# A fused attention and causal-convolution kernel: where the sums of weights and of outputs stand among a softmax's steps, and where its reciprocal and division stand

## The chip, the cores and the metric

The kernel runs on one core of a Trainium2 chip. A core has a matrix engine (TensorE, PE in the profile; PEld is its weight load), a vector engine (VectorE, DVE), a scalar engine (ScalarE, ACT), a general engine (GpSimd, POOL) and a queue engine that issues DMAs (SyncE, SP). Each runs its own instructions in order and waits for the others by semaphores. The metric is device time in microseconds, the median of several runs. Everything is float32.

## The reference

For four sequences (b) of 1024 tokens with 1024 channels and 16 heads of 64:

```python
scale, shift = split(cond @ W_emb + b_emb)             # one row a sequence
xn  = rms_norm(x, g_norm) * (1 + scale) + shift
q, k, v = heads(xn @ W_qkv)                            # (b, 16, 1024, 64)
q, k = rms_norm(q, g_q), rms_norm(k, g_k)
o   = softmax(q @ k.T / 8) @ v                         # heads joined again
x   = x + (o + o @ W_out)
x   = x + causal_conv(x, taps=cond, bias=b)            # depthwise, 4 taps
```

The last layer takes the four rows of cond as the taps of a depthwise convolution over tokens.

## The kernel before

**Products.** Both large products (with W_qkv and with W_out) are done as two-by-two blocks in seven multiplications instead of eight, which needs sums and differences of blocks. Those of x go to DRAM as scrA (L326), those of W_qkv as scrB (class Weights, combine, L565, four subtractions of 128x384 for each of four row blocks of a double), those of W_out as scrW (class OutWeights: diagonals L908, two of 128x128, and combine L916, four of 128x512), those of o as scrS (class OutSums, combine, L942, four of 128x512). In this document "a lot" is one such group of two or four instructions on DVE. A later load (w_P, wq_P, o_P) brings the results back.

**Stages.** A "double" is two pairs of heads: 28 pieces of four matmuls (L648), each into a PSUM tile of the pool ps_m, which has three buffers in turn. DVE and ACT empty such tiles (L658 to L669); qk is scaled on DVE (L498) and transposed on PE (L506). The same three buffers serve qkt, the transposes of x (xtp), the output product's po and pe (L1046, emptied for example by L1058, L1077 and L1080), and the sums' tot (L767).

**Units.** A unit is one pair of heads and one half of the queries; there are 64, 16 a sequence. Its steps: eight score tiles on PE (L689), copied by ACT to sp (L697); eight maxima, of which seven instructions on DVE (L706); the maximum over partitions on POOL (L711); its copy to PSUM by ACT (mbp, L720); eight shifts on DVE (L725); eight exponentials on ACT (L729); seven additions of the exponentials on POOL (L731); and in the next unit's time the product with v (pav, L752, a PSUM tile with one buffer), the total over partitions (tot, L767), then the reciprocal and the division. The reciprocal's way: ACT copies tot to tots (L785), a DMA spreads it over 128 partitions as few (L787), DVE takes the reciprocal of 128x8 (L790), a DMA writes it to DRAM (scrR, L792), and two DMAs read it back as rec (L795), each row of it on 64 partitions. The division oT = pav * rec follows on DVE (L804) and a DMA stores it (L811).

**Order.** For PE, DVE, ACT and POOL, the order of instructions on an engine is the order in which the Python code issues them. A model clock orders it: `tick(us)` advances it by the time of PE's work, `defer(delay, key, step)` runs a step once the clock has passed, and `need(key)` runs at once whatever still waits under a key. The `softmax` method (L733) of a unit sets, counted from its call: the maximum over partitions at 2.6 (TO_MAX), the copy at 6.5 (TO_SPREAD), shift kt at 7.6 + kt times 1.8 (TO_SHIFT, STEP; 1.6 in the first sequence), the exponential 1.3 behind it. `finish` (L763) defers the copy of tots by 0.2 and `invert` (the reciprocal and its two DMA steps) by 6.0; this is called one pair of score tiles before `softmax`. `divide` is deferred by DIVIDE = 15.0 from `softmax`.

Work without a due time of its own, the lots (but for the first few) and most scalings of qk, is handed in with `defer_gap`. `fill_gap(GAP)` takes what is ripe, scalings of qk first, up to 6.5 us by estimate, and is called at TO_MAX + 0.1, while POOL takes the maximum.

SP issues all DMAs, in an order of its own; a DMA at the head of its queue that waits holds back the ones behind it.

Of the kernel before, what the change touches and what calls it, by code (L numbers as in the profile page):

```python
# [21 lines left out]
def kernel(  # L22
# [69 lines left out]
    clock = [0.0]  # L92
# [3 lines left out]
    def defer(delay, key, step):  # L96
        pending.append((clock[0] + delay, next(serial), key, step))

    def flush(due):
        while True:  # L100
            ready = [e for e in pending if due(e)]
            if not ready:
                return
            entry = min(ready, key=lambda e: e[:2])
            pending.remove(entry)
            entry[3]()

    def tick(us):

        clock[0] += us  # L110
        flush(lambda e: e[0] <= clock[0])
# [4 lines left out]
    idle, loud = [], [0.0, 0.0]  # L116
# [3 lines left out]
        pending.append(entry)  # L120
        idle.append((clock[0] + delay, us, entry))

    def fill_gap(us):
        for e in sorted(idle, key=lambda e: e[2][2][0] != "qk"):
            if e[2] not in pending:
                idle.remove(e)
            elif e[0] <= clock[0] and e[1] <= us:
                us -= e[1]
                idle.remove(e)
                pending.remove(e[2])  # L130
                e[2][3]()
# [8 lines left out]
    def need(*key):  # L140
        flush(lambda e: e[2] == key)
# [535 lines left out]
    class Unit:  # L677
# [55 lines left out]
        def softmax(self):  # L733

            key = ("exp", self.name)
            loud[0] = clock[0] + TO_SHIFT + TO_EXP
            step = STEP if self.pr.b else STEP_FIRST
            loud[1] = loud[0] + NT * step + LOUD
            defer(TO_MAX, key, self.maximum)
            defer(TO_MAX + 0.1, key, lambda: fill_gap(GAP))  # L740
            defer(TO_SPREAD, key, self.broadcast)
            for kt in range(NT):
                at = TO_SHIFT + kt * step
                defer(at, key, lambda kt=kt: self.shift(kt))
                defer(at + TO_EXP, key, lambda kt=kt: self.weigh(kt))
# [15 lines left out]
        def finish(self):  # L761
            b, c = self.pr.b, self.pr.c
            tot = ps_m.tile([P, HN], F32, tag="m", name=f"tot_{self.name}")  # L763
            for g in range(4):
                h, i = divmod(g, 2)
                some = slice(0, HN) if self.final else slice(i * QN, (i + 1) * QN)
                nc.tensor.matmul(  # L767
                    tot[32 * g : 32 * (g + 1), : some.stop - some.start],
                    ones,
                    self.sum[:, h, some],  # L770
                    start=True,
                    stop=True,
                )
            tick(2 * PAIR)
            self.tot = tot
            if self.final:
                return
            key = ("tot", self.name)
            defer(0.2, key, lambda: self.spread(tot))
            defer(6.0, key, self.invert)  # L780

        def spread(self, tot):

# [417 lines left out]
    TO_MAX, TO_SPREAD, TO_SHIFT, TO_EXP, STEP = 2.6, 6.5, 7.6, 1.3, 1.8  # L1201
# [1 line left out]
    SHARES = (0.25, 0.5, 0.25)  # L1203
    LEADS = ((11, 7), (10, 9))
    LEADS_LAST = ((11, 7), (10, 12))
    DIVIDE = 15.0
    STEP_FIRST = 1.6
    BEHIND_FIRST = 22.0
    LATER = ((0, 0), (4, 0))
    GAP = 6.5  # L1210
    AGE = 30.0
    LOUD = 5.0
    PB = NJ // 2
# [182 lines left out]
    def between(p):  # L1396

        b, i = divmod(p, NB)
        slots = [[] for _ in range(7)]
        for j in range(7):  # L1400
            T = 7 * (p + 4) + j
            slots[j] = piece(T) if T < ND * NPR + 16 else []
        slots[0].append((0.0, lambda: store(AGE)))
        d, k = divmod(p - 11, NB)
        if 0 <= d < B - 1 and k % 2 == 0 and k < NJ:
            slots[0].append((0.0, lambda: OutSums(d, k // 2).load()))
        if p < NB + 1:
            for i in PLAN.get(p, ()):
                slots[0] += [(0.0, lambda: load_step(i)), (0.0, lambda: load_o(i))]
        if p == NB + 1:  # L1410
            for load in (lambda: load_step(KH), lambda: load_o(KH), lambda: load_step(KH + 1)):
                slots[0].append((0.0, load))
        for a, pieces in enumerate(out_steps(p)):
            slots[(2, 5)[a] if NB < p < B * NB - 4 else 6] += pieces
        if p == B * NB - 4:
            slots[0].append((0.0, lambda: held.load(0, 0)))
            slots[0].append((0.0, lambda: held.load(1, 0)))
            slots[6].append((0.0, lambda: defer(1.0, ("S3",), held.differences)))
        if p == B * NB - 2:
            slots[6].append((0.0, lambda: defer(5.0, ("o2",), lambda: held.load(0, 1))))  # L1420
            slots[6].append((0.0, lambda: defer(5.0, ("o2",), lambda: held.load(1, 1))))
            slots[6].append((0.0, lambda: defer(11.0, ("S1",), lambda: held.sums((0, 1), range(KH - 1)))))
        if p == B * NB - 1:
            slots[6].append((0.0, lambda: defer(1.0, ("S4",), lambda: held.sums((2,), range(KH - 1)))))
        return [piece for slot in slots for piece in slot]
# [19 lines left out]
    def split(pieces, behind):  # L1445

        left, n = behind, len(pieces)
        while n and left > 0:
            n -= 1
            left -= pieces[n][0]  # L1450
        return cut(pieces[:n], SHARES) + [pieces[n:]]
# [38 lines left out]
    last = None  # L1490
    for p in range(B * NB):
        unit = Unit(doubles[p // 4].pairs[p // 2 % 2], p % 2)
        stretches = split(between(p), BEHIND if p else BEHIND_FIRST)
        stretches = iter(stretches)

        def fill():
            run(next(stretches))

        if last is not None:
            need("exp", last.name)  # L1500
            last.values(range(0, HT))
        unit.scores((0, 1))
        fill()
        if last is not None:
            last.values((4, 5))
        unit.scores((2, 3))
        fill()
        if last is not None:
            last.values((6, 7))
        unit.scores((4, 5))  # L1510
        fill()
        if last is not None:
            last.finish()
        unit.scores((6, 7))
        need("mx", unit.name)
        unit.softmax()
        if last is not None:
            defer(DIVIDE, ("oT", last.pr.b, last.pr.c, last.half), last.divide)
        fill()
        last = unit  # L1520
# [45 lines left out]
```

## Time and profile before

| what | value |
|---|---|
| median of 3 runs | 2849.01 us (2847.79 to 2849.99) |
| the profiled execution | 2850.03 us, span 2848.2 us |
| PE busy | 2744.6 us, 96% of the span |
| DVE busy | 2217.1 us, 78% |
| ACT, POOL busy | 1539.2 us, 1325.5 us |
| chain that ended last | PE 72%, DVE 14%, DMA 7% |
| mean TensorE clock granted | 0.993 |
| POOL's additions, L731 | 384 of 2.44 us, 64 of 2.37 us in the mean |
| shifts, L725 | 512 of 1.21 us |
| division, L804 | 64, median 0.683 us |

How to read it: busy time counts an engine's instructions that run, not those that wait, issue DMAs or handle semaphores. In a timeline, a row has the start, the length, the engine, the line, what is written and read, the shape and the number of instructions merged in it; in brackets stands the engine's idle time before the row and what ended it. A group of a tile's view has the least, the median and the greatest length of one instruction in ns. In a table of windows, the columns are the busy time of each engine with the number of its instructions, then the granted share of TensorE's clock, the DMA engines' busy share and GB/s.

### The profile page before, as it was taken

To read this page: it belongs to the slowest core of one execution; us is meant where nothing else is said; L and a number is where in the kernel's file an instruction comes from. 1 tells how busy PE (TensorE), PEld (TensorE's weight loads), DVE (VectorE), ACT (ScalarE), POOL (GpSimd) and SP (SyncE) were. 2 spreads that over 40 slices of the span, in tenths; PEclk is the share of its full clock that TensorE was granted. 3 is DMA by queue.
4 is the path that set the end of the run, shared out by engine and by line. 5 is a ranking of instruction groups with operands and counts; after the bars stand their busy time and mean duration, and the time that the engine had idled before them with its cause. 6 is when DMAs were issued, how large, how long until landed. Compare 5 with 4: busy or idle time off the path is not lost.

```text
span 2848.2 us, 31740 instructions
## 1 busy us (share of the span) xinstructions
PE 2744.6 (96%) x10533; PEld 1304.7 (46%) x10533; DVE 2217.1 (78%) x2623; ACT 1539.2 (54%) x2208; POOL 1325.5 (47%) x534
## 2 busy tenths in 40 slices
PE   6999999999999999999999999999999999999978
PEld 3544444444444444444444445444444444443334
DVE  4587787877887887878788778777887887788786
ACT  4255656655555656655555556665454545555532
POOL 2055544554455544544554555354455445544520
PEclk9999999999999999999999999999999999999999
DMA  9854556655545655754554556565456444534554
GB/s 322 272 167 144 192 165 206 215 180 173 172 164 173 207 188 186 243 171 165 188 196 158 172 196 194 189 210 194 152 176 218 140 146 163 170 126 137 174 155 122
DMA packets 420503, 518.31 MB, mean 182 GB/s; under 512 B 40884, under 2 KB 323572, under 8 KB 410996
## 3 DMA queue, kind: packets, MB, share of 16 engines
q1 hardware_dynamic: 420340, 516.29, 55.5%
q8 instruction: 84, 1.38, 0.2%
q14 instruction: 79, 0.65, 0.1%
HBM read 417.63 MB, written 98.30 MB: 181 GB/s over the span
## 4 chain that ended last, share of the span: by engine, by line
PE 72%; DVE 14%; DMA 7%; ACT 3%; issue 2%; SPq 1%; POOL 0%; DVEq 0%; ACTq 0%; POOLq 0%
PE pqkv_P L648 28%; PE pav L752 15%; PE s L689 14%; DVE mx L706 5%; PE po_P L1046 5%; PE po L1046 4%; DVE sp L725 2%; DVE qk L498 2%; DMA rec<-scrR 2%; PE pe_P L1046 1%; DMA scrR<-few 1%; PE qkt L506 1%; ACT sp L697 1%; DVE S L942 1%; DMA we<-in_L_cond_W_emb_dram 1%
## 5 line engine op out<-in xcount | busy, mean ns | idle before, releaser
L648 PE MATMUL pqkv_P<-w_P,a 128*128 128x384 f32 x3456 | 1178.0, 491 | 29.2 <-issue 6.6
L731 POOL TENSOR_TENSOR sum<-sum,sp 128x1024 f32<-128x1024 f32 x384 | 936.8, 2440 | 42.5 <-ACT sp L729 13.3
L648 PEld LDWEIGHTS pqkv_P<-w_P,a 128*128 128x128 f32 x3456 | 641.2, 191 | 494.3 <-issue 80.6
L697 ACT COPY sp<-s 128x1024 f32<-128x1024 f32 x512 | 501.4, 1016 | 495.3 <-PE s L689 494.9
L729 ACT ACTIVATE sp<-sp 128x1024 f32<-128x1024 f32 x512 | 533.3, 1055 | 229.1 <-DVE sp L725 224.3
L725 DVE TENSOR_TENSOR sp<-sp,mbp 128x1024 f32<-128x1024 f32 x512 | 607.2, 1211 | 27.2 <-ACT mbp L720 27.2
L711 POOL PARTITION_ALL_REDUCE mb<-mx x64 | 219.7, 3433 | 852.5 <-DVE mx L706 454.0
L706 DVE TENSOR_TENSOR mx<-mx,sp 128x1024 f32<-128x1024 f32 x384 | 484.8, 1262 | 126.6 <-ACT sp L697 96.3
L689 PE MATMUL s<-qT,kT 64*128 64x512 f32 x2048 | 510.6, 617 | 3.1 <-ACT sp L697 3.1
L752 PE MATMUL pav<-sp,v 128*64 128x512 f32 x2048 | 482.0, 602 | 4.3 <-DVE oT L804 4.3
L731 POOL TENSOR_TENSOR sum<-sp,sp 128x1024 f32<-128x1024 f32 x64 | 151.4, 2366 | 483.7 <-ACT sp L729 223.7
L689 PEld LDWEIGHTS s<-qT,kT 64*128 64x128 f32 x2048 | 175.8, 186 | 307.6 <-ACT sp L697 143.2
L1169 DVE SCALAR_TENSOR_TENSOR y<-x,cols,y 128x512 f32<-128x512 f32 x192 | 276.6, 1444 | 16.1 <-ACT y L1157 11.5
L752 PEld LDWEIGHTS pav<-sp,v 128*64 128x64 f32 x2048 | 130.4, 136 | 322.6 <-issue 292.9
L706 DVE TENSOR_TENSOR mx<-sp,sp 128x1024 f32<-128x1024 f32 x64 | 109.7, 1714 | 161.2 <-ACT sp L697 161.1
L1046 PE MATMUL po_P<-o_P,wq_P 128*128 128x512 f32 x352 | 158.3, 594 | 6.7 <-DMA o_P<-scrS 2.6
L667 DVE TENSOR_TENSOR qk<-u,pqkv_P 128x256 f32<-128x256 f32 x256 | 105.4, 412 | 76.0 <-PE pqkv_P L648 76.0
L498 DVE TENSOR_TENSOR qk<-qk,ms 128x1024 f32<-128x1024 f32 x64 | 136.0, 2145 | 0.0
L1046 PE MATMUL po<-o_P,wq_P 128*128 128x512 f32 x288 | 129.8, 593 | 2.8 <-DMA o_P<-scrO 1.8
L720 ACT COPY mbp<-mb 128x1024 f32<-128x1024 f32 x64 | 65.1, 1017 | 117.8 <-POOL mb L711 117.8
L1157 ACT ACTIVATE y<-x,cols,tap_self 128x512 f32<-128x512 f32 x64 | 52.1, 813 | 119.4 <-DVE x L1080 117.5
L1046 PEld LDWEIGHTS po_P<-o_P,wq_P 128*128 128x128 f32 x352 | 65.6, 190 | 81.2 <-issue 66.3
(118 smaller groups left out, 1810.4 us busy)
## 6 DMA issues: line engine op xcount, KB each, us to landing
a<-scrA SPq DMA_DIRECT2D x212, 512.0 KB
w_P<-scrB SPq DMA_DIRECT2D x64, 768.0 KB
o_P<-scrS SPq DMA_DIRECT2D x44, 1024.0 KB
w_P<-in_L_cond_W_qkv_dram SPq DMA_DIRECT2D x192, 192.0 KB
o_P<-scrO SPq DMA_DIRECT2D x29, 1024.0 KB
wq_P<-scrW SPq DMA_DIRECT2D x108, 256.0 KB
scrA<-r SPq DMA_DIRECT2D x28, 896.0 KB
xc<-in_x_dram SPq DMA_DIRECT2D x64, 256.0 KB
```

The costliest lines, as they stand in the source:

```text
L498: nc.vector.tensor_mul(qk, qk, self.ms[g].unsqueeze(2).to_broadcast([P, 4 * HT, D]))
L648: nc.tensor.matmul(pm, (chunk.r(place) if a is None else a[:, k, :])[:, t % 2 * P : (t % 2 + 1) * P], w[:, k, :], start=(k == 0), stop=(k ...
L689: nc.tensor.matmul(ps[:, h, :], pr.kT[kt // HT][h * D : (h + 1) * D, kt % HT * P : (kt % HT + 1) * P], pr.qT[self.half][h * D : (h + 1) * ...
L697: nc.scalar.copy(sp, ps)
L706: nc.vector.tensor_max(self.mx, self.mx if kt > 1 else self.sp[0], self.sp[kt])
L711: nc.gpsimd.partition_all_reduce(self.mb.rearrange("p h q -> p (h q)"), self.mx.rearrange("p h q -> p (h q)"), P, bass_isa.ReduceOp.max,)
L725: nc.vector.tensor_sub(self.sp[kt], self.sp[kt], self.mb)
L729: nc.scalar.activation(sp, sp, AF.Exp)
L731: nc.gpsimd.tensor_tensor(self.sum, self.sum if kt > 1 else self.sp[0], sp, ALU.add)
L752: nc.tensor.matmul(self.pav[h * D : (h + 1) * D, :], self.pr.v[kt // HT][:, kt % HT, h * D : (h + 1) * D], self.sp[kt][:, h, :], start=(kt ...
L1046: nc.tensor.matmul(pm, self.w[name][:, k, :], self.operand(name, k), start=start and k == 0, stop=k == KH - 1)
L1169: nc.vector.scalar_tensor_tensor(self.y, self.x1[:, k : k + HN], cols[:, r : r + 1], self.y, ALU.mult, ALU.add)
```

## The change

```diff
-    def fill_gap(us):
-        for e in sorted(idle, key=lambda e: e[2][2][0] != "qk"):
+    def fill_gap(us, scales):
+        for e in list(idle):
             if e[2] not in pending:
                 idle.remove(e)
-            elif e[0] <= clock[0] and e[1] <= us:
+            elif e[0] <= clock[0] and e[1] <= us and (e[2][2][0] == "qk") == scales:
...
-            defer(TO_MAX + 0.1, key, lambda: fill_gap(GAP))
+            defer(TO_MAX + 0.1, key, lambda: fill_gap(GAP, True))
+            defer(TO_SHIFT + 2.0 * STEP + 0.1, key, lambda: fill_gap(GAP, False))
...
-            defer(6.0, key, self.invert)
+            defer(9.0, key, self.invert)
...
-    DIVIDE = 15.0
+    DIVIDE = 12.0
...
-    GAP = 6.5
+    GAP = 5.0
...
         need("mx", unit.name)
+        if last is not None:
+            need("tot", last.name)
         unit.softmax()
```

`fill_gap` is now called twice in a unit: at the old place for scalings of qk alone, and 0.1 behind the due time of the third shift for everything else, with 5.0 us by estimate each. The `need("tot")` ahead of `softmax` issues the reciprocal and its DMA steps directly behind the eighth maximum of the next unit, before anything that `softmax` defers; the 9.0 of `finish` is thus never reached there. The division comes due at 12.0 instead of 15.0 behind `softmax`, which is behind the third shift instead of the fifth, and behind the lots where there are any.

The order of instructions, compared engine by engine, is the same on PE, ACT and POOL; it differs on DVE and SP. In the first sequence and a little beyond, each of the first 19 units held one or two lots ahead of its first shift; after the change 16 of the first 18 hold one or two, behind the third shift (the first unit's behind the first). In the second and third sequence, four lots of o each stood in every second unit (eighth maximum at 1260.9, 1343.2 and so on) and now stand one unit earlier (1221.0, 1304.2 and so on), behind the third shift.

## The prediction

> **What bounds the kernel now.** I read the page first, then the waits of TensorE and of VectorE, then the timelines of single units. The page says that TensorE is busy nearly all the span:
>
> ```profile
> PE 2744.6 (96%) x10533; PEld 1304.7 (46%) x10533; DVE 2217.1 (78%) x2623; ACT 1539.2 (54%) x2208; POOL 1325.5 (47%) x534
> ```
>
> So 2848.2 - 2744.6 = 104 us are idle on PE, and a change that adds no PE work can win part of that at most. In the windows of 100 us, PE is busy 92.7 to 97% between 100 and 900 us, and 96.5 to 100% from 900 to 2700. Other engines matter only where they make PE wait, and VectorE (DVE) is the one that does, because it empties PE's PSUM tiles. Among DVE's own waits this one belongs to the change:
>
> ```profile
> DVE oT L804 <- DMA rec<-scrR: 52.4, 20, 5.0
> ```
>
> The division waits 20 times for the reciprocals' way through DRAM. The timeline of DVE shows how in a unit that holds sums (I name a unit by the end of its eighth maximum; here 1260.9):
>
> ```profile
> 1260.82 4.05 DVE L498 TENSOR_TENSOR qk<-qk,ms 128x1024 f32<-128x1024 f32 x2
> 1264.80 2.86 DVE L942 TENSOR_TENSOR S<-S 128x512 f32<-128x512 f32 x4
> 1267.57 0.20 DVE L790 RECIPROCAL few<-few 128x8 f32<-128x8 f32 x1
> 1267.68 1.17 DVE L725 TENSOR_TENSOR sp<-sp,mbp 128x1024 f32<-128x1024 f32 x1
> ...
> 1273.82 1.21 DVE L725 TENSOR_TENSOR sp<-sp,mbp 128x1024 f32<-128x1024 f32 x1
> 1278.32 0.69 DVE L804 TENSOR_TENSOR oT<-pav,rec 128x512 f32<-128x512 f32 x1 [3.29 <-DMA rec<-scrR]
> ```
>
> The reciprocal stands behind the sums, 6.7 us after the maximum; the issues of scrR and rec follow at 1268.36 and 1272.79, between loads, and DVE idles 3.29 us with three shifts queued behind the division. The change takes this stall away.
>
> **What goes.** "tots" is copied and "few" issued 2.5 us ahead of the eighth maximum's end (1258.44 here), and where the reciprocal stood first after it, at +0.4 us, it didn't wait. So moved forward it costs its 0.19 us and no wait. Of SP's queue: scrR (0.4 us) and the two rec issues (0.6 each) move up some 3 to 6 us past one or two loads of w_P and a, which PE releases anyway; where nothing lay between, SP went from scrR to rec in 1.4 us (scrR's landing); rec landed 5.5 us after its first issue here, so at some +7.5 us, and the division comes at +9 or later. I take the 52.4 us of DVE's wait as gone (both ends: all of it, or half if the queue is full). What that is worth on PE: in eleven units the trace has a PE gap at +17 to +22 us (starts of matmuls against their usual spacing), behind the late division or the shifts that it held up (1.43, 1.25, 0.74, 1.49, 0.87, 0.61, 1.59, 0.43, 1.96, 1.91, 1.21), 13.5 us in all. In the first batch, sums ahead of the first shift also hold up DVE's emptying of PSUM: at 656.95 PE waited 1.69 us for u of L660, which stood behind 4.9 us of W sums. Gaps of this kind there are about 14 us; I take 8. **Gain 21.5 us** (bounds 13 and 27).
>
> **What comes.** PE's, ACT's and POOL's orders stay as they are; DVE's and SP's change. Sums stood ahead of shift 0, while POOL ran its all-reduce (3.25 us), and there one of them took 0.69 us. Now they stand behind shift 2. The nearest rows for what they meet there are these two groups of the same shape, both with two SBUF inputs:
>
> ```profile
> L942 DVE TENSOR_TENSOR S<-S x48: 677/692/2385, 616.4 to 2180.2; 128x512 f32<-128x512 f32 x48
> L853 DVE TENSOR_TENSOR S<-o,o x4: 776/2840/2853, 2601.3 to 2607.5; 128x512 f32<-128x512 f32 x4
> ```
>
> The four of L853 are the only ones that ran beside POOL's additions (L731, 2.37 us each): three took 2.84 us, waiting out one addition apiece. The shifts (an input in PSUM) take 1.21 us beside POOL and without. When do the additions start? In every unit at +10.4 to +12.8 us. Behind the third shift of a unit that is the moment the sums arrive. But POOL has only two additions to do until shift 3 is through, as the third needs its exponential. So a lot of four costs 4 x 0.69 = 2.8 us of work plus up to two waits of 2.1, **7 us**.
>
> Worked out for the unit at 1221.0, which now holds the S lot that the unit at 1260.9 held:
>
> ```profile
> 1231.20 1.21 DVE L725 TENSOR_TENSOR sp<-sp,mbp 128x1024 f32<-128x1024 f32 x1
> 1232.33 0.68 DVE L1077 TENSOR_TENSOR ou<-ou_P,po_P 128x512 f32<-128x512 f32 x1
> 1232.92 2.34 DVE L725 TENSOR_TENSOR sp<-sp,mbp 128x1024 f32<-128x1024 f32 x2
> 1235.19 0.68 DVE L804 TENSOR_TENSOR oT<-pav,rec 128x512 f32<-128x512 f32 x1
> 1235.79 0.41 DVE L667 TENSOR_TENSOR qk<-u,pqkv_P 128x256 f32<-128x256 f32 x1
> ```
> ```profile
> 1231.33 2.37 POOL L731 TENSOR_TENSOR sum<-sp,sp 128x1024 f32<-128x1024 f32 x1 [6.88 <-ACT sp L729]
> ```
> ```profile
> 1230.93 5.32 PE L648 MATMUL pqkv_P<-w_P,a 128*128 128x384 f32 x16
> 1236.09 0.60 PE L506 MATMUL qkt<-ident,qk 128*128 128x128 f32 x4
> 1236.53 2.78 PE L648 MATMUL pqkv_P<-w_P,a 128*128 128x384 f32 x8
> ```
>
> POOL has begun at 1231.33, before shift 2 ends at 1232.4. The lot ends near 1238.7, then oT 0.6, then L1077 until 1239.9 instead of 1233.0. It empties the PSUM tile whose buffer (three of ps_m, in turn) the transposes at 1236.09 take: PE waits 3.7 us. Then two shifts, and L667 ends at 1242.5 (before 1236.3) for the product at 1236.53: 2 us more. Together 6.
>
> A unit where shift 2 ends before POOL starts is better off: at 1304.2 shift 2 ends at +8.8 and POOL starts at +10.6, so three sums are free and one waits: x of L1080 is 3.7 us late, with 2.1 to spare, PE waits 1.7. Done so for each unit that now holds sums, shift 0 moved up to the end of the broadcast copy where sums had held it: 1.0, 3.4, 5.1, 3.5, 5.1, 1.0, 4.8, 7.4, 5.8, 4.4 in the first batch (units at 140, 213, 254, 367, 408, 487, 531, 572, 690, 727; the other first-batch lots stay within their cover) and 6.4, 1.7, 5.8, 1.7, 5.8, 2.1, 5.4, 2.5 in the later two (every second unit from 1221 to 1508.6 and 1889.6 to 2174.9; a few steps of 0.2 included). That is **73 us**. If each lot met one addition only, ten of these would be 2 to 3 us smaller: 43. I take the middle, **58**, as both the start of POOL and who gets in first at the meeting are uncertain by about one sum.
>
> A long PE gap costs more. At 230.03 PE had idled 3.07 us, and the next eight matmuls took 5.46 us instead of the 2.75 of other rows of eight:
>
> ```profile
> 230.03 5.46 PE L648 MATMUL pqkv_P<-w_P,a 128*128 128x384 f32 x8 [3.07 <-DVE sp L725]
> ...
> 229.00:236.00 7.00, 5.97 (x10) 2.82 (x12) 3.79 (x6) 3.87 (x7) 6.76 (x4) 0.52 1.03 318
> ```
>
> The granted clock is 0.52 in that stretch and 0.66 at 317 to 322, after a gap of 2.47 us; after 1.69 us (656.95) it stays 1.00. Of the gaps above, twelve exceed 2.5 us, and two of these units pay already: 10 x 2.6 = 26 us at most; for the middle case I count six, **16 us** (8 at the low end). The Trainium skill ("TensorE: Matmul & The Clock Gate", part 1) halves the clock after an idle window of about 3.4 us that runs free of the work; by it, an estimate, gaps of 2.5 us would mostly go free and this term would be about half. The row at 317 speaks against that.
>
> **Sum**: 58 + 16 - 21.5 = +52 us on the profiled execution's 2850.0 (span 2848.2), 2902; the runs' median is 1 us lower: **2901 us**. Bounds: 73 + 26 - 13 = +86 and 43 + 8 - 27 = +24, so 2935 and 2873.
>
> **The rivals.** (1) *The sums go through together*: they stand 0.03 us apart, and if DVE runs a lot without a break and POOL waits instead, a lot costs 2.8 us less the 0.7 of the division that leaves its old place. The slacks of PSUM tiles in these stretches are 0.1 to 4.6 us, so PE loses perhaps 0.5 us in each of the 24 units that hold sums, 12 us, against 21.5 gained: 2850.0 - 9.5 is 2840. It decides from a PE loss below 0.9 us a unit. For it: the 0.03 us gaps. Against: L853, whose sums stand as close, and the taps of L1169, which take 2.7 us beside POOL and 0.75 alone. Chance 0.13. (2) *The cover is better than I read it*: DVE idles between the shifts and the next scores (1.52 us at 1242.37), few gaps reach 2.5 us, the gains are whole: +0 to +22, about 2862. Chance 0.15, of which 0.07 lies within 0.2%. (3) *The reciprocal waits for few*: behind it stand qk scaling and PSUM's emptying. Landing 1 us after the maximum would cost up to 0.5 us of PE in 63 units, +30 on top: about 2930. Against it: no wait in the trace at +0.4. Chance 0.05. My forecast has 0.67.
>
> Slower by over 0.2% (about what a measurement of this kernel can tell from no change): 0.67 + 0.05 + 0.08 = 0.80; within: 0.07; faster: 0.13. The range, 2858 to 2935, leaves out rival 1 and the smallest losses.
>
> **What would show it.** Right: sums of L565, L916 and L942 near 2.5 us in mean where two meet POOL, the wait of oT for rec nearly gone, PE gaps of 2 to 6 us at +12 to +18 in the units named, and stretches with a clock of about 0.5 behind them. Wrong: sums at 0.69 us, or an unchanged PE beside late DVE work, or a wait of the reciprocal for its DMA.

## The result, and the profile after

The changed kernel takes **2929.2 us** in the median of 4 runs (2924.4 to 2932.7), the kernel before, run beside it, 2849.5 (2847.8 to 2850.6): a ratio of 1.0279, 95% interval 1.0261 to 1.0297. The forecast was 2901 with a range of 2858 to 2935. The time came out slower, as forecast, and inside the range, but +80 us where the sum gave +52. One run of the kernel before, in the last set of runs, took 3589 us at a mean clock of 0.782; it is left out of all comparisons here.

The profiled execution took 2929.29 us, its span is 2927.5. The page's line of busy times:

```profile
PE 2772.1 (95%) x10533; PEld 1317.2 (45%) x10533; DVE 2283.5 (78%) x2623; ACT 1544.0 (53%) x2208; POOL 1346.2 (46%) x534
```

Against before, PE is busy 27.5 us more with the same 10533 matmuls (a lower clock: mean 0.98 against 0.993), and idle 155.4 us instead of 103.6. So of the span's +79.3, 51.8 are new idle time and 27.5 slower matmuls. DVE is busy 66 us more with the same 2623 instructions: the sums have become longer by 33.7 us in all, the maxima (L706), which have two SBUF inputs as well, by 26.3. The groups of the same shape as before's L942 and L916 (one line lower now; least, median, greatest in ns):

```profile
L943 DVE TENSOR_TENSOR S<-S x48: 684/692/2821, 611.1 to 2220.6; 128x512 f32<-128x512 f32 x48
L917 DVE TENSOR_TENSOR W<-W x16: 685/692/2828, 563.0 to 782.1; 128x512 f32<-128x512 f32 x16
```

Most are still 0.69 us. The long ones are few, and come at most twice in a lot. The unit that stood at 1221.0 has its eighth maximum at 1269.0 now. Its DVE, POOL and PE timelines:

```profile
1268.90 0.20 DVE L791 RECIPROCAL few<-few 128x8 f32<-128x8 f32 x1
...
1279.14 1.22 DVE L725 TENSOR_TENSOR sp<-sp,mbp 128x1024 f32<-128x1024 f32 x1
1280.27 6.49 DVE L943 TENSOR_TENSOR S<-S 128x512 f32<-128x512 f32 x4
1286.67 0.68 DVE L805 TENSOR_TENSOR oT<-pav,rec 128x512 f32<-128x512 f32 x1
1287.27 0.68 DVE L1078 TENSOR_TENSOR ou<-ou_P,po_P 128x512 f32<-128x512 f32 x1
1287.87 2.35 DVE L725 TENSOR_TENSOR sp<-sp,mbp 128x1024 f32<-128x1024 f32 x2
1290.13 0.42 DVE L667 TENSOR_TENSOR qk<-u,pqkv_P 128x256 f32<-128x256 f32 x1
1290.46 0.28 DVE L667 TENSOR_TENSOR v<-u,pqkv_P 128x128 f32<-128x128 f32 x1
```
```profile
1279.64 2.35 POOL L731 TENSOR_TENSOR sum<-sp,sp 128x1024 f32<-128x1024 f32 x1 [7.17 <-ACT sp L729]
1282.08 2.68 POOL L731 TENSOR_TENSOR sum<-sum,sp 128x1024 f32<-128x1024 f32 x1
1290.32 4.81 POOL L731 TENSOR_TENSOR sum<-sum,sp 128x1024 f32<-128x1024 f32 x2 [5.57 <-ACT sp L729]
```
```profile
1278.95 5.32 PE L648 MATMUL pqkv_P<-w_P,a 128*128 128x384 f32 x16
1288.01 0.66 PE L506 MATMUL qkt<-ident,qk 128*128 128x128 f32 x4 [3.73 <-DVE ou L1078]
1290.84 5.25 PE L648 MATMUL pqkv_P<-w_P,a 128*128 128x384 f32 x8 [2.18 <-issue]
```

The lot of four takes 6.49 us: 2.28, 2.72, 0.69 and 0.69. It waits out what is left of POOL's first addition and then the second, which in turn runs 0.33 us late (2.68 against 2.35); the third addition can't come, because shift 3 stands behind the lot. PE waits 3.73 us for the tile that L1078 empties, and 2.18 us more until just behind the end of L667 at 1290.74 (the profile names no releaser there), where the prediction had 3.7 and 2. The next eight products take 5.25 us instead of 2.75. This unit is 8.8 us longer.

What the change was to take away is gone: the division's wait for rec (52.4 us, 20 times) is in no row of DVE's waits, and the reciprocal never waited (L791, mean 196 ns). In DVE's list another wait has grown; columns are total, times and longest, here of the kernel after:

```profile
DVE mx L706 <- ACT sp L697: 255.3, 123, 11.7
DVE qk L667 <- PE pqkv_P L648: 87.8, 60, 7.0
DVE sp L725 <- ACT mbp L720: 61.7, 51, 4.2
```

The first shift waits 61.7 us for the broadcast maximum, where it was 27.2 us, 28 times, before. That is the cover under which the lots used to run, now left empty.

The lengths of the units (end of one eighth maximum to the next) add up as follows, in us against before's trace. "Eight lots" are the units at 1221, 1304, 1388, 1470, 1890, 1972, 2055 and 2137, which hold a lot in the changed kernel; "eight freed" are the ones that follow them, which held it before. "Last three units" are those at 2582, 2626 and 2668. Stretches that change little are left out, so a row's parts need not reach its span. The rows below the first belong to the experiments. A row is one execution: those of "after, additions short", "lots back, reciprocal early" and "lots back, division late" are the fastest of their runs, 3, 7 and 7 us below the medians given further on.

| kernel (profiled execution) | first 18 units | eight lots | eight freed | last three units | behind the last maximum | span |
|---|---|---|---|---|---|---|
| after | +46.2 | +31.6 | -9.0 | +10.2 | -3.3 | +79.3 |
| before, additions short | -12.4 | -0.4 | +2.4 | -3.2 | -10.9 | -20.5 |
| after, additions short | -22.0 | +9.3 | -7.7 | +3.2 | -8.3 | -24.4 |
| lots back, reciprocal early | -4.2 | +0.7 | -8.0 | +10.8 | -3.1 | -0.6 |
| lots back, reciprocal early, division late | -5.8 | +1.2 | -8.2 | +8.6 | -4.5 | -5.6 |
| lots back, reciprocal early but for the last four units | -2.1 | 0.0 | -6.7 | +4.6 | -2.8 | -5.5 |
| lots alone | +34.0 | +33.6 | -9.2 | +3.1 | -1.9 | +60.1 |
| the change but for the last four units | +49.9 | +30.4 | -9.0 | -0.3 | 0.0 | +74.3 |
| lots behind the eighth shift | +14.0 | +12.5 | -10.0 | +12.2 | -2.7 | +31.7 |
| lots behind the second shift | +16.1 | +19.9 | -10.1 | +9.7 | -1.3 | +40.6 |
| early reciprocal in eight units | -9.8 | +0.2 | -7.3 | +2.5 | +0.9 | -11.2 |

The eight lots differ, and their units with them. Four lots (units at 1221, 1388, 1890, 2055) met additions: they took 4.94 to 6.92 us, and their units became 5.8 to 8.8 us longer, 29.5 in all. The other four (1304, 1470, 1972, 2137) stood behind the same shift but ended before POOL began: they took 2.87 us, and their units became 0.3 to 1.1 us longer, 2.1 in all.

### The profile page after: what moved, and what is told of

Same layout as the page of the kernel before. It is cut to its first block, busy times and chain, and to the rows that moved or that the text cites. A ratio compares the mean times of both kernels' runs of the same rounds, so it can differ in the third digit from the quotient of the medians.

```text
span 2927.5 us, 31695 instructions
## 1 busy us (share of the span) xinstructions
PE 2772.1 (95%) x10533; PEld 1317.2 (45%) x10533; DVE 2283.5 (78%) x2623; ACT 1544.0 (53%) x2208; POOL 1346.2 (46%) x534
## 4 chain that ended last, share of the span: by engine, by line
PE 70%; DVE 17%; POOL 3%; issue 3%; DMA 3%; ACT 3%; SPq 1%; DVEq 0%; POOLq 0%; ACTq 0%
PE pqkv_P L648 31%; PE s L689 12%; PE pav L753 12%; DVE mx L706 5%; PE po_P L1047 5%; PE po L1047 4%; DVE sp L725 3%; DVE y L1170 2%; POOL sum L731 2%; PE qkt L506 1%; PE pe_P L1047 1%; DVE r L326 1%; POOL mb L711 1%; PE tot L768 1%; DMA we<-in_L_cond_W_emb_dram 1%
## 5 line engine op out<-in xcount | busy, mean ns | idle before, releaser
L648 PE MATMUL pqkv_P<-w_P,a 128*128 128x384 f32 x3456 | 1193.5, 496 | 48.8 <-issue 23.9
L731 POOL TENSOR_TENSOR sum<-sum,sp 128x1024 f32<-128x1024 f32 x384 | 952.3, 2480 | 96.5 <-ACT sp L729 68.2
L648 PEld LDWEIGHTS pqkv_P<-w_P,a 128*128 128x128 f32 x3456 | 650.1, 193 | 521.2 <-issue 105.1
L725 DVE TENSOR_TENSOR sp<-sp,mbp 128x1024 f32<-128x1024 f32 x512 | 606.6, 1216 | 61.7 <-ACT mbp L720 61.7
L706 DVE TENSOR_TENSOR mx<-mx,sp 128x1024 f32<-128x1024 f32 x384 | 503.1, 1310 | 124.3 <-ACT sp L697 93.4
L1170 DVE SCALAR_TENSOR_TENSOR y<-x,cols,y 128x512 f32<-128x512 f32 x192 | 278.9, 1456 | 16.3 <-ACT y L1158 11.8
L706 DVE TENSOR_TENSOR mx<-sp,sp 128x1024 f32<-128x1024 f32 x64 | 117.7, 1839 | 161.9 <-ACT sp L697 161.9
L667 DVE TENSOR_TENSOR qk<-u,pqkv_P 128x256 f32<-128x256 f32 x256 | 105.5, 412 | 90.0 <-PE pqkv_P L648 87.8
```

The lines of the kernel that those rows point to most:

```text
L648: nc.tensor.matmul(pm, (chunk.r(place) if a is None else a[:, k, :])[:, t % 2 * P : (t % 2 + 1) * P], w[:, k, :], start=(k == 0), stop=(k ...
L706: nc.vector.tensor_max(self.mx, self.mx if kt > 1 else self.sp[0], self.sp[kt])
L725: nc.vector.tensor_sub(self.sp[kt], self.sp[kt], self.mb)
L731: nc.gpsimd.tensor_tensor(self.sum, self.sum if kt > 1 else self.sp[0], sp, ALU.add)
L1170: nc.vector.scalar_tensor_tensor(self.y, self.x1[:, k : k + HN], cols[:, r : r + 1], self.y, ALU.mult, ALU.add)
```

## The experiments

My theory after the result: the 80 us come from DVE's sums meeting POOL's additions with PSUM's emptying queued behind them; the early reciprocal works against that. The rivals: the early reciprocal and division cost the time (order of DMAs), or the new place costs it whatever POOL does.

**Additions cut short, before and after.** POOL's additions 1 to 6 of a unit add 64 of 1024 columns; only the last is whole, so the totals aren't the reference's. Order and number of instructions stay. The same edit in the kernel before and in the changed one:

```diff
-                nc.gpsimd.tensor_tensor(self.sum, self.sum if kt > 1 else self.sp[0], sp, ALU.add)
+                some = slice(0, HN if kt == NT - 1 else 32)
+                nc.gpsimd.tensor_tensor(self.sum[:, :, some], self.sp[0][:, :, some], sp[:, :, some], ALU.add)
```

In the kernel before:

> The kernel before with six of POOL's seven additions of a unit cut to 64 of 1024 columns; only the last one is whole. The totals are therefore not those of the reference. It serves as the base of the next kernel. Theory: nothing moves by much, since lots stand beside the all-reduce here; only the taps and maxima that met additions get shorter: 2835 to 2850 us. Rival theories say the same of it.

In the changed kernel:

> The changed kernel with the same cut of POOL's additions (the totals are not those of the reference). Theory (it is the meeting with whole additions that costs): a lot behind the third shift takes 2.8 us instead of some 7, PE's gaps in the units with lots go, and the kernel is level with or faster than the one before with the same cut: between -20 and +8 us against it. Rival (the lots' own work in the midst of the shifts is what DVE cannot take, POOL or not): +40 us or more against it.

Measured: 2829.3 us and 2829.0 us, ratios to before 0.9938 (0.9923 to 0.9953) and 0.9936 (0.9918 to 0.9954). The first came out lower than expected: its first 18 units gain 12.4 us and the end of the program 10.9. But the two stand level: **the +80 us between the kernels goes when the additions are short.** The same unit's DVE row and its POOL rows, in the changed kernel with short additions:

```profile
1211.05 2.91 DVE L944 TENSOR_TENSOR S<-S 128x512 f32<-128x512 f32 x4
```
```profile
1210.79 0.31 POOL L732 TENSOR_TENSOR sum<-sp,sp 128x64 f32<-128x64 f32 x1 [7.54 <-ACT sp L729]
1212.36 0.32 POOL L732 TENSOR_TENSOR sum<-sp,sp 128x64 f32<-128x64 f32 x1 [1.26 <-ACT sp L729]
```

The lot stands in the same place, behind the same shift, at the same moment as POOL's first addition, and takes 2.91 us. Not all of the place's price is gone: the eight lots, now of 2.9 to 3.0 us, still cost 9.3 us in the table, 1.1 to 3.8 in each of the units at 1221, 1388, 1890 and 2055; the freed units and the first 18 balance that. But what made it +80 is the additions. The edit does more than part the lots from the additions: in the kernel before, where the lots met none, DVE is busy 168.8 us less with it (2048.3 against 2217.1), 111.7 of them in the taps of the convolution (y, L1169 there), so DVE has more time to spare as well. That the meeting itself counts shows in the changed kernel without any such edit, in the 29.5 us of the four units whose lots met additions against the 2.1 us of the four whose lots met none. The Trainium skill ("SBUF — State Buffer", SBUF: two separate sides) says that a DVE operation with two SBUF inputs and a GpSimd operation that reads SBUF lock each other out for a whole instruction. These rows agree: 0.69 us against 2.72 us, the second being 2.03 us longer, where one addition takes 2.35.

**One part alone.** The lots put back to the old place, reciprocal and division left early ("the reciprocal alone" below):

```diff
-            defer(TO_SHIFT + 2.0 * STEP + 0.1, key, lambda: fill_gap(GAP, False))
+            defer(TO_MAX + 0.1, key, lambda: fill_gap(GAP, False))
```

> The changed kernel with the lots of sums back ahead of the first shift, each in the unit where it stood before the change; the early reciprocal and the early division stay. Theory (the lots meet POOL's additions behind the third shift, DVE falls behind, PSUM tiles come free late and PE waits): the loss is gone and the gain of the early reciprocal is left, 2828 to 2842 us, below the kernel before (2849.5). Rival (the early reciprocal, the division and the DMA issues that moved with them on SP's queue bear a part, for example the 10 us that the changed kernel loses in the units from 2582 us of the trace before on): 2855 us or more.

Measured: 2856.1 us (2849.4 to 2858.9, 10 runs), 1.0024 (1.0013 to 1.0035). My theory missed, as it expected a gain; the rival's side held. **Reciprocal and division early, without the lots' move, are 7.5 us slower, not 21.5 faster.** And the other half, lots behind the third shift, reciprocal and division where they were:

```diff
-            defer(9.0, key, self.invert)
+            defer(6.0, key, self.invert)
...
-    DIVIDE = 12.0
+    DIVIDE = 15.0
...
-        if last is not None:
-            need("tot", last.name)
         unit.softmax()
```

> The other half: the lots stand behind the third shift as in the changed kernel, and the reciprocal (due at 6.0) and the division (15.0) stand as before the change. Theory: the whole loss without the gain, 2935 to 2950 us, over the changed kernel's 2929. Rival (the early reciprocal bears a part): below the changed kernel, 2900 to 2925.

Measured: 2906.7 us (2904.9 to 2910.1), 1.0206 (1.0189 to 1.0224), a miss again: less than after, not more. So: lots alone +58.1, reciprocal alone +7.5, both +79.7, which is 14 more than their sum. The table and PE's waits bear on that. The eight freed units gain 8.0 with the early reciprocal, 9.2 with the lots moved, 9.0 with both: it is one gain, since either parts the reciprocal from the lot that stood ahead of it. And PE's waits for the last addition grow faster than the parts; the rows of the changed kernel, of the lots alone and of the reciprocal alone:

```profile
PE tot L768 <- POOL sum L731: 14.3, 6, 4.1
```
```profile
PE tot L768 <- POOL sum L731: 5.4, 5, 2.2
```
```profile
PE tot L768 <- POOL sum L731: 5.7, 5, 2.4
```

It was 1.0 us before; so both together add 13.3 us, the parts 4.4 and 4.7. My reading is that both edits push shifts and with them POOL's additions back, until the last one ends behind the moment that tot asks for it. The remainder of the 14 I can't place.

**Where the early reciprocal loses.** In its trace the loss stands in the last three units (+10.8). SP's queue in the second of these, with the lots back and the reciprocal early, then before:

```profile
2619.81 0.32 SPq L793 DMA_DIRECT2D scrR<-few  x1
2620.18 0.43 SPq L1192 DMA_DIRECT2D out_dram<-ot  x1
2621.25 1.11 SPq L796 DMA_DIRECT2D rec<-scrR  x2
2622.45 0.54 SPq L1192 DMA_DIRECT2D out_dram<-ot  x1
2623.08 0.46 SPq L999 DMA_DIRECT2D wq_P<-scrW  x1
2623.59 0.66 SPq L1026 DMA_DIRECT2D o_P<-scrS  x1
```
```profile
2626.66 0.34 SPq L792 DMA_DIRECT2D scrR<-few  x1
2627.09 0.39 SPq L1191 DMA_DIRECT2D out_dram<-ot  x1
2628.12 1.11 SPq L795 DMA_DIRECT2D rec<-scrR  x2
2629.32 0.54 SPq L998 DMA_DIRECT2D wq_P<-scrW  x1
2629.90 0.50 SPq L1025 DMA_DIRECT2D o_P<-scrS  x1
```

Behind rec, one more output store now stands ahead of the loads. In the third of these units the reciprocal's steps pass loads; rec and a load of xc, with the reciprocal early, then before:

```profile
2669.20 1.10 SPq L796 DMA_DIRECT2D rec<-scrR  x2
2670.34 0.59 SPq L1121 DMA_DIRECT2D xc<-in_x_dram  x1
```
```profile
2670.07 0.50 SPq L1120 DMA_DIRECT2D xc<-in_x_dram  x1
2673.59 1.11 SPq L795 DMA_DIRECT2D rec<-scrR  x2
```

Some of what PE waits for, over the whole span, in the first of the two kernels and before:

```profile
PE po_P L1047 <- DMA o_P<-scrS: 4.0, 1, 4.0
PE po L1047 <- DMA o_P<-scrO: 2.2, 1, 2.2
PE pe_P L1047 <- DMA wq_P<-scrW: 1.9, 1, 1.9
PE po L1129 <- DMA xc<-in_x_dram: 11.2, 4, 4.4
```
```profile
PE po_P L1046 <- DMA o_P<-scrS: 2.6, 2, 1.9
PE po L1128 <- DMA xc<-in_x_dram: 7.2, 4, 3.6
```

In the last three units alone PE's waits for loads are 9.6 us (the first three rows and 1.5 us for xc), against 2.3 before (1.9 for o_P, 0.4 for xc). Where rec passed xc, xc is issued 3.2 us behind the eighth maximum instead of 1.9. In the unit at 2626, the load of o_P is issued no later than before (3.9 us behind the maximum, 4.0 before), and PE waits for it 2.1 us longer; that the store ahead of it is the reason isn't shown. Whether it takes the early division too, the next kernel tests: the one with the lots back, with only the division at 15.0 again.

```diff
-    DIVIDE = 12.0
+    DIVIDE = 15.0
```

> The early reciprocal alone: lots ahead of the first shift as before the change, division due at 15.0 as before the change. The kernel with both early (e1_sums_back) took 7 us more than the kernel before; its trace is shorter in the units that hold lots from 1260 us on (by 8 us) and longer by 11 us in the three units from 2582 us on, where PE waits for loads of o_P, xc and wq_P. Theory (the reciprocal's DMA issues, moved up, change SP's order there): the loss at the end stays, 2850 to 2858 us. Rival (the early division and its store do it): it goes, 2838 to 2846 us.

Measured: 2851.5 us, 1.0009 (0.9995 to 1.0023), inside the expected range: the last three units still lose 8.6, so that loss needs no early division. But the interval holds 1, so over the whole program this kernel can't be told from the one before. Then, on the kernel with the lots back, the last four units in before's order:

```diff
-            defer(9.0, key, self.invert)
+            defer(6.0, key, self.invert)
...
-        if last is not None:
+        early = p < B * NB - 4
+        if last is not None and early:
             need("tot", last.name)
         unit.softmax()
         if last is not None:
-            defer(DIVIDE, ("oT", last.pr.b, last.pr.c, last.half), last.divide)
+            defer(DIVIDE if early else 15.0, ("oT", last.pr.b, last.pr.c, last.half), last.divide)
```

> Lots ahead of the first shift as before the change; reciprocal and division early in all units but the last four, where both stand as before the change. Theory (the gain of the early reciprocal is there, in the units with lots, and is given back in the last units alone): 2838 to 2846 us, faster than the kernel before (2849). Rival (the early reciprocal costs a little in every unit): 2849 to 2856 us.

Measured: 2844.6 us, 0.9987 (0.9973 to 1.0002): inside the theory's numbers, but its interval touches 1, and 4.6 us of the loss are still in the last three units. There PE's waits for loads have gone from 9.6 to 0.6 us, which fits the order of DMAs as their cause; of what is left, 4.0 us wait for DVE (2.7 for L725, 1.3 for L1059). And the same edit on the changed kernel:

> The changed kernel, lots behind the third shift, but reciprocal and division of the last four units at before's places (due 6.0 and 15.0). Theory: the 10.3 us that the units at 2582, 2626 and 2668 lost in the changed kernel come from the reciprocal's DMA issues alone and add to the rest: 2919 us, 2914 to 2923. Rival: the last units are late because of what the lots left behind (loads and stores that pile up), and keep their loss: 2926 to 2932.

Measured: 2926.6 us, 1.0265 (1.0251 to 1.0278), against 1.0279 for the whole change: by the time this is the rival's number. By the trace it is the theory's mechanism: the last three units stand at -0.3 instead of +10.2. My expectation had left out that the stretch behind the last maximum gives 3.3 us back in the changed kernel and nothing here, so at most 7 us were to be had; the spans differ by 5.0, as the first 18 units came out 3.7 us longer.

**Another place for the lots.** Behind the eighth shift, in the middle of the additions, the early reciprocal kept:

```diff
-            defer(TO_SHIFT + 2.0 * STEP + 0.1, key, lambda: fill_gap(GAP, False))
+            defer(TO_SHIFT + 7.0 * STEP + 0.1, key, lambda: fill_gap(GAP, False))
```

> The changed kernel with the lots behind the eighth shift instead of the third; nearly all lots then stand amid POOL's additions, of which four or more are left, so each sum waits for one, 11 us a lot instead of 3 to 9. Theory (what counts is what stands behind the lots on DVE: shifts and the emptying of PSUM tiles that PE needs next): little of that is left behind the eighth shift, so less loss although there are more waits, 2855 to 2915 us. Rival (each wait for POOL costs by itself): more than the changed kernel, 2930 to 2990 us.

Measured: 2881.1 us, 1.0111 (1.0091 to 1.0131). A lot of it:

```profile
1257.40 9.95 DVE L943 TENSOR_TENSOR S<-S 128x512 f32<-128x512 f32 x4
1267.28 0.41 DVE L667 TENSOR_TENSOR qk<-u,pqkv_P 128x256 f32<-128x256 f32 x1
```

**These lots are the longest of all, 9 to 11 us, and cost less than half**: 12.5 us in the eight units, where lots of 2.9 to 6.9 us cost 31.6, and 14.0 in the first 18 instead of 46.2. No shift stands behind them, only a little emptying of PSUM. So a wait of the sums costs little by itself and much by what is queued behind it. Length counts too: in the four units at 1304, 1470, 1972 and 2137, where the changed kernel's lots met no addition and cost 2.1 us, these long ones cost 7.9. Behind the second shift instead (1.0 in place of 7.0 in the same line):

> The changed kernel with the lots behind the second shift. There they start at about +7.5 to +9 us behind the maximum, and POOL's first addition starts at +10.4 or later. Theory: most sums run at their 0.69 us, a lot costs 2.8 us and seldom one wait of 2, and most of the loss goes: 2852 to 2880 us. Rival (it is the work in the midst of the shifts that costs): near the changed kernel, 2910 to 2930 us.

Measured: 2888.9 us, 1.0136 (1.0114 to 1.0159), 9 us above what the theory allowed. Six of the eight lots there meet no addition (2.9 us long), two meet one (4.9 us), and the eight units lose 19.9. Of these, 13.0 stand in the two units whose lot met an addition (7.2 at 1221, 5.8 at 1890), 7.0 in the other six, 0.0 to 2.1 each. So the meetings that the theory called seldom make most of the price, even one a lot, and a lot that meets none costs little even in the midst of the shifts.

**A version that beats both.** Lots and qk's scaling at the old place, the reciprocal early only in the eight units where a lot stood ahead of it and a gain was seen:

```diff
-            defer(TO_SHIFT + 2.0 * STEP + 0.1, key, lambda: fill_gap(GAP, False))
+            defer(TO_MAX + 0.1, key, lambda: fill_gap(GAP, False))
...
-            defer(9.0, key, self.invert)
+            defer(6.0, key, self.invert)
...
+        early = p in (2, 6, 28, 30, 32, 34, 46, 50)
-        if last is not None:
+        if last is not None and early:
             need("tot", last.name)
         unit.softmax()
         if last is not None:
-            defer(DIVIDE, ("oT", last.pr.b, last.pr.c, last.half), last.divide)
+            defer(DIVIDE if early else 15.0, ("oT", last.pr.b, last.pr.c, last.half), last.divide)
```

> The kernel before, with the reciprocal (and its DMAs) directly behind the next unit's eighth maximum and the division at 12.0 in eight units only, those at 213, 367, 1261, 1343, 1426, 1509, 2010 and 2175, which hold a lot ahead of their first shift; everywhere else, the order of before. Theory: the early reciprocal gains where a lot stood ahead of it and loses elsewhere by its DMAs' places in SP's queue (in the units at 177, 331, 531 and in the last three). With the gains of those eight units alone, 4.7 + 4.7 + 8.2 = 17.6 us by the unit lengths of the kernel with the lots back: 2831 us, 2826 to 2838. Rival: the units' lengths shift gaps and do not remove them (what one unit wins the next loses): 2843 to 2852.

Measured: **2837.0 us** (2833.3 to 2842.7) against 2851.1 of before beside it: 0.9952 (0.9939 to 0.9965). It is the fastest complete kernel of this study, 0.5% ahead of before, and inside the theory's range; the rival, that gaps only shift, fell. Its unit at 1261 (1253.4 here), on DVE:

```profile
1253.42 0.20 DVE L791 RECIPROCAL few<-few 128x8 f32<-128x8 f32 x1
1253.54 4.01 DVE L498 TENSOR_TENSOR qk<-qk,ms 128x1024 f32<-128x1024 f32 x2
1257.47 2.86 DVE L943 TENSOR_TENSOR S<-S 128x512 f32<-128x512 f32 x4
1260.24 1.22 DVE L725 TENSOR_TENSOR sp<-sp,mbp 128x1024 f32<-128x1024 f32 x1
...
1264.76 0.68 DVE L805 TENSOR_TENSOR oT<-pav,rec 128x512 f32<-128x512 f32 x1
```

The reciprocal runs ahead of scaling and lot, and the division finds rec there, without the 3.29 us of before.

## Why the prediction was right, and where its size was off

The direction and the mechanism of the loss were right. That the time fell inside the range owes something to luck: a gain of 21.5 us didn't come, the clock cost 11.5 us more than the sum had and tot's waits weren't counted, all on the same side, and +80 lies close to the upper bound of +86.

- **DVE bounds PE through PSUM's emptying**: right. 51.8 us of the new time are PE idle, at the gaps named (3.73 and 2.18 us in the unit worked out).
- **Up to two waits a lot, since POOL has two additions before shift 3**: right, without exception in the trace: of the 28 lots behind a third shift eight have two sums longer than 1 us, eight have one, twelve have none, and no lot has a third. So rival 1, that the sums go through together, fell: sums 0.03 us apart still let POOL's next addition in between.
- **Lots, 58 us**: of the right size, with errors that cancel. In the four units at 1221, 1388, 1890 and 2055, the working at two waits gave 23.4 us of gaps, and with up to 2.6 us of clock each 34; measured, +29.5. The ten units named in the first batch gave 41.5; measured 42.5, clock and gains in it. So there the upper bound was nearer than the middle. But at 1304, 1470, 1972 and 2137 the forecast had one wait and 8.0 us; POOL started there at +11.8 to +13.4 instead of +10.6, no sum waited, and the four units lost 2.1. The term counts PE's idle time, and lengths of units have the clock in them; what it came to by itself isn't measured. In the kernel with the lots alone, PE idles 39.6 us more and is busy 20.5 us longer; the eight freed units' gain of 9.2 us is already in that. One reading behind the term was too kind to the old place: the prediction gives a sum beside the all-reduce 0.69 us, but in the kernel before the first sum of a lot that stood right behind the maximum took 2.1 to 2.4 us (units at 177, 331, 650, 690, 805 and 2010).
- **Clock, 16 us**: too small; PE's busy time rose by 27.5. A row after a long gap in the changed kernel, and the window behind it (busy times, then clock, DMA share and GB/s):

```profile
616.78 4.37 PE L648 MATMUL pqkv_P<-w_P,a 128*128 128x384 f32 x8 [6.62 <-issue]
```
```profile
616.50:620.00 3.50, 3.22 (x5) 1.85 (x6) 3.50 (x7) 1.56 (x3) 0.36 (x1) 0.51 0.77 302
1290.80:1296.50 5.70, 5.66 (x13) 3.33 (x14) 4.24 (x7) 3.20 (x4) 5.54 (x3) 0.57 0.95 298
```

  The low clock follows gaps of 6.62 us and also two gaps of 3.73 and 2.18 us with four short matmuls between them. The rule of the Trainium skill ("TensorE: Matmul & The Clock Gate", Part 1) that the prediction weighed would have made the term about 8 by the prediction's own estimate; the measured rise went the other way.
- **Gain, 21.5 us: this step failed.** DVE's wait of 52.4 us went as said, but what it was worth on PE didn't come: "reciprocal alone" is +7.5 us in the medians, and -0.6 in the profiled execution, where gains and losses are level. Its gains in the trace are 4.7 us each in the units at 213 and 367 and 8.0 us in the eight freed, some 17; they are lost again in the last three units (+10.8) and in several units of the first batch (the units at 177, 331 and 531 are 1.6 to 2.0 us longer; in the first two PE waits 2.4 and 2.0 us for POOL's last addition, 0.7 and 0.4 before, so there it isn't the loads). The prediction's sentence that scrR and rec move "past one or two loads of w_P and a, which PE releases anyway" looked at the stretch of that one unit; the end of the program, where stores and megabyte loads stand behind them, was not read. And part of the gain isn't the reciprocal's: with the lots moved away it comes by itself (9.2 us). The trace of the kernel with the lots back is of its fastest run, 7 us below its median; what the slower ones lose is in no trace.
- **Not in the sum at all**: tot's waits for POOL's last addition, 13.3 us more than before, in six units up to the one at 805. The prediction followed the late shifts to PE's scores and PSUM, not to ACT's exponentials and POOL.
- **Rival 3**, a reciprocal that waits for few: no such wait. **Rival 2**, better cover: it happened in the four units that start late, not elsewhere.

## What to carry to other kernels

Judge a place for filler work by what is queued behind it and by what it will meet there, and not only by how long the filler runs: the longest lots here, some 10 us, cost 0.4 to 2.9 us a unit at the end of the shifts; those of 4.9 to 6.9 us that met additions in the middle of the shifts cost 5.8 to 8.8; and those of 2.9 us that met none there, 0.3 to 1.1 (up to 3.8 where only short additions ran). A stall that can be removed by parting two instructions should be removed at the few places where they meet; done everywhere, the same move also shifted DMAs in a shared queue, and won nothing. When two edits remove the same stall, count the gain once, and measure each alone.

## What the runs showed of the hardware

- A DVE sum of 128x512 with two SBUF inputs takes 0.69 us, and up to 2.83 when it meets POOL's additions of 2.35 us; in the unit at 1221 POOL's addition then took 2.68. There the two engines took turns, one instruction each (2.28 and 2.72 us of DVE's, 2.35 and 2.68 of POOL's), although the sums stand in the queue one directly behind the other. With POOL's additions at 0.31 us it is back at 0.69 (mean of L944 over the 48 of that kernel: 0.695 us). The shifts, with an input in PSUM, took 1.20 to 1.22 us in both kernels.
- Eight matmuls of 128x384 took 4.37 us after a gap of 6.62, and 5.25 us after gaps of 3.73 and 2.18 us, against 2.75: the longer gap had the smaller price.
